# Attention probabilities: the multiply by the reciprocal sum, from VectorE to ScalarE

## The chip, the core and the metric

The kernel runs on one core of one Trainium2 chip. The metric is device time in microseconds (us), taken as the median of several runs; lower is better. The profile is of one execution on the same kind of core. The engines are called PE (TensorE, matrix products), DVE (VectorE), ACT (ScalarE), POOL (GpSimd) and SP (SyncE, which issues most of the transfers). PEld is PE's loading of weights, which overlaps its products.

## What is computed

Two blocks of a network act on x, eight batches of 512 tokens with 256 channels. Block 0 adds a state-space layer (a recurrence over time, behind several exponential moving averages) and then a mixture of 8 experts. Block 1 adds an attention layer and then a mixture of 32 experts. The change touches the attention alone:

```python
Q = (x @ Wq.T).reshape(b, n, H, R)        # H = 8 heads, R = 64
K = (x @ Wk.T).reshape(b, n, H, R)
V = (x @ Wv.T).reshape(b, n, H, d)        # d = 256
attn = jnp.einsum('bnhr,bmhr->bhnm', Q, K)
attn = jax.nn.softmax(attn, axis=-1)      # 512 x 512 for each batch and head
out = jnp.einsum('bhnm,bmhd->bnd', attn, V)
```

Everything is in 32-bit floats here.

## The kernel before

Activations lie with channels on the 128 partitions and the 512 tokens of a batch along the free axis, so a tile of 128 x 512 holds half the channels of one batch.

Two threads of work are issued interleaved. Thread X does the state-space layer, batch after batch. Its inner loop has 64 items for each batch: ACT makes dA, an exponential (line 623), POOL makes h, a product (625), DVE runs a scan along time (651) and a multiply (652), and PE folds the result (660). Beside it X does the moving averages of the next batch, scans and multiply-adds on DVE (475 to 485). Thread Y does, for a group of batches, the mixture of 8 experts and then the low-rank layer and the attention. The groups are batch 0; 1 and 2; 3, 4 and 5; 6 and 7. Y of one group runs beside X of the next. Y of the last group has no X beside it; it runs beside the routing of the second mixture (function top4). Behind all that come the 95 tiles of the 32 experts and the output. Each engine executes its instructions in the order in which they were laid down; the framework's scheduler settles that order when the program is built, from the interleaved emission, and it gives copies issued on "any" engine to ACT or DVE.

The attention of one batch runs over four pairs of heads (line 862). For each pair:

- Lines 868 to 871 make Q and K of both heads (tile qk, copied from PSUM by "any" engine).
- `scores(i)`, for each of four blocks of 128 queries and both heads u: PE makes 128 x 512 scores in a PSUM tile (888), DVE takes the row maximum nm (892), ACT takes the exponential and, in the same instruction, its row sum den (895), DVE takes the reciprocal of den (896) and multiplies ex by it in place (897). Tile ex has four buffers, den and nm have four each.
- `values(i)` makes V on PE and copies it from PSUM (879, "any" engine).
- `turn(i)` transposes ex on PE in four pieces (905) and copies the result from PSUM into aT (906, "any" engine).
- Line 922 multiplies V by aT on PE, in 32 matmul instructions a pair, and line 926 adds the sums to x.

Score tiles come from a PSUM pool g of two buffers, the values, transposes and outputs from a pool acc of two buffers. A score buffer is free again once the exponential has read it; an acc buffer once the copy has. Line 897 runs 256 times in all: 8 batches x 4 pairs x 4 blocks x 2 heads.

Of the kernel before, what the change touches and what calls it, by code (L numbers as in the profile page):

```python
# [12 lines left out]
AF = mybir.ActivationFunctionType  # L13
ALU = mybir.AluOpType
# [37 lines left out]
def adaln_attn_ffn_kernel(ctx: ExitStack, tc: tile.TileContext, d: dict, out: bass.AP):  # L52
    nc = tc.nc
# [22 lines left out]
    def mm(o, pairs):  # L76
        for i, (lhsT, rhs) in enumerate(pairs):
            nc.tensor.matmul(o, lhsT, rhs, start=(i == 0), stop=(i == len(pairs) - 1))  # L78
# [632 lines left out]
    def thread_y(q, bs, ps):  # L711
# [4 lines left out]
        def g():  # L716
            return ps.tile([P, T], F32, tag="g", name="g", bufs=2)

        def acc():
            return ps.tile([P, T], F32, tag="acc", name="acc", bufs=2)  # L720
# [94 lines left out]
        with ExitStack() as ph:  # L815
            wk = ph.enter_context(tc.tile_pool(name=f"k3_{q}", bufs=1))
            H = 8
            for r, b in enumerate(bs):
# [43 lines left out]
                for hp in range(H // 2):  # L862
                    wqk = wk.tile([P, 2, KC, P], F32, tag="wqk", name="wqk")
                    nc.sync.dma_start(wqk, d["wqk"][hp])
                    wv = wk.tile([P, KC, T], F32, tag="wv", name="wv", bufs=1)
                    nc.sync.dma_start(wv, d["Wv"][hp])
                    qk = wk.tile([P, 2, T], F32, tag="qk", name="qk")
                    for u in range(2):
                        pt = g()
                        mm(pt, [(wqk[:, u, k, :], c[:, k, :]) for k in range(KC)])  # L870
                        nc.any.tensor_copy(qk[:, u, :], pt)  # L871
                    yield 4
                    aTs = [wk.tile([P, 4, T], F32, tag=f"aT{u}", name=f"aT{u}") for u in range(2)]
                    V = wk.tile([P, 4, T], F32, tag="V", name="V")

                    def values(m):
                        pt = acc()
                        mm(pt, [(c[:, k, ts(m, P)], wv[:, k, :]) for k in range(KC)])
                        nc.any.tensor_copy(V[:, m, :], pt)  # L879

                    exs = {}

                    def scores(i):

                        sps = [g() for u in range(2)]
                        for u in range(2):
                            r0 = 64 * u
                            mm(sps[u], [(qk[r0 : r0 + 64, 0, ts(i, P)], qk[r0 : r0 + 64, 1, :])])
                        for u in range(2):
                            sp = sps[u]  # L890
                            nm = wk.tile([P, 1], F32, tag="nm", name="nm", bufs=4)
                            nc.vector.tensor_reduce(nm, sp, AX.X, ALU.max, negate=True)  # L892
                            ex = wk.tile([P, T], F32, tag="ex", name="ex", bufs=NEX)
                            den = wk.tile([P, 1], F32, tag="den", name="den", bufs=4)
                            nc.scalar.activation(ex, sp, AF.Exp, bias=nm, accum_out=den)  # L895
                            nc.vector.reciprocal(den, den)
                            nc.vector.tensor_scalar(ex, ex, den, None, ALU.mult)
                            exs[i, u] = ex

                    def turn(i):  # L900
                        for u in range(2):
                            tp = acc().rearrange("p (m t) -> p m t", m=4)
                            ex = exs.pop((i, u))
                            for m in range(4):
                                nc.tensor.transpose(tp[:, m, :], ex[:, ts(m, P)], ident)  # L905
                            nc.any.tensor_copy(aTs[u][:, :, ts(i, P)], tp)  # L906

                    for i in range(4):
                        scores(i)
                        yield 2  # L910
                        values(i)
                        yield 2
                        if i > 0:
                            turn(i - 1)
                            yield 2
                    turn(3)
                    yield 2
                    ys = [acc() for k in range(KC)]
                    for k in range(KC):
                        for u in range(2):  # L920
                            for m in range(4):
                                nc.tensor.matmul(  # L922
                                    ys[k], V[:, m, C * u + P * k : C * u + P * (k + 1)], aTs[u][:, m, :],
                                    start=(u == 0 and m == 0), stop=(u == 1 and m == 3))
                            yield 3.5
                        nc.vector.tensor_tensor(x[:, k, :], x[:, k, :], ys[k], ALU.add)
# [274 lines left out]
```

## Time and profile before

| | |
|---|---|
| median of 3 runs | 4290.34 us (4277.67 to 4293.29) |
| the profiled execution, time | 4282.53 us |
| the profiled execution, span of the page | 4280.8 us |
| mean granted PE clock | 0.886 of full speed |
| L895 on ACT, exponential, 128x512 | 256 times, 686 ns, 175.0 us |
| L896 on DVE, reciprocal, 128x1 | 256 times, 154 ns, 39.2 us |
| L897 on DVE, multiply, 128x512 | 256 times, 628 ns, 160.5 us |
| L906 on ACT, copy of aT from PSUM | 189 times, 586 ns, 108.3 us |
| L906 on DVE, copy of aT from PSUM | 67 times, 682 ns, 45.4 us |
| L879 on ACT, copy of V from PSUM | 93 times, 580 ns, 53.9 us |
| L879 on DVE, copy of V from PSUM | 35 times, 686 ns, 24.0 us |
| L623 on ACT, exponential with a scale tile | 512 times, 720 ns, 360.5 us |
| L651 on DVE, scan | 512 times, 1585 ns, 799.0 us |
| table loads on ACT | 284 |

In a line of the profile stand the source line, engine and operation, the tiles written and read with their shapes, and the count; then the busy time in us and the mean of one in ns; then the idle time of the engine just before these instructions, with the releaser that ended most of it. The rows of digits cut the span in 40 equal slices; each digit is the busy share of a slice in tenths. In the timeline a line gives start, length, engine, source line, operation and count, and in brackets the idle time before it and what ended it. One 32-bit matmul on 512 columns shows as two instructions.

### The profile page before, as it was taken

The numbers are of one execution on the slowest core, as the hardware profiler recorded it, in microseconds if no ns is written. First come the engines' busy times: TensorE is split into PE (matmuls) and PEld (weight loads), VectorE is DVE, ScalarE is ACT, GpSimd is POOL, SyncE is SP. The second block draws the span as 40 slices with busy tenths as digits, with TensorE's granted clock in tenths as the row PEclk, the third lists the DMA queues.
The fourth block names the chain that finished last, engine by engine and source line by source line (L and its number), as shares of the span: only waits on it lengthen the run. The fifth ranks groups of instructions, "written<-read, shape, count | busy, mean of one in ns | idle before, by whom it ended". The sixth has DMA issues, their size and how long they took to land. (4 is left out here: it accounts for less than half of the span.)

```text
span 4280.8 us, 36836 instructions
## 1 busy us (share of the span) xinstructions
PE 3470.1 (81%) x10964; PEld 1699.2 (40%) x10964; DVE 2667.8 (62%) x4276; ACT 1683.1 (39%) x2753; POOL 1570.6 (37%) x1222
## 2 busy tenths in 40 slices
PE   4557686888687888888858898889988999977994
PEld 2111352332254233333327443333456444436773
DVE  5698957987866686796791547565432354443336
ACT  2535463454355345346433443332223243222222
POOL 0456535435536334433552323231043211124552
PEclk7668798898798898999879998999999999989996
DMA  3325445234446423333346312213043212117776
GB/s 104 120 91 194 180 153 172 99 116 165 161 162 210 140 100 117 128 117 106 138 169 226 125 62 70 74 35 104 15 160 137 90 44 70 36 44 243 249 239 221
DMA packets 159372, 554.78 MB, mean 130 GB/s; under 512 B 27730, under 2 KB 34289, under 8 KB 146756
## 3 DMA queue, kind: packets, MB, share of 16 engines
q1 hardware_dynamic: 135076, 501.35, 34.8%
q0 software_dynamic: 24096, 51.08, 3.2%
q8 instruction: 87, 1.43, 0.1%
q14 instruction: 113, 0.93, 0.1%
HBM read 453.00 MB, written 234.82 MB: 161 GB/s over the span
## 5 line engine op out<-in xcount | busy, mean ns | idle before, releaser
L625 POOL TENSOR_TENSOR h<-packed,B 128x512 f32<-128x512 f32 x512 | 790.7, 1566 | 1045.0 <-PE yp L660 669.6
L651 DVE TENSOR_TENSOR_SCAN h<-dA,h 128x512 f32<-128x512 f32 x512 | 799.0, 1585 | 142.8 <-POOL h L625 77.3
L623 ACT ACTIVATE dA<-packed,Aexp 128x512 f32<-128x512 f32 x512 | 360.5, 720 | 676.5 <-DVE h L651 468.1
L160 POOL DMA_INDIRECT tok<-ys,to_i x310 | 312.5, 1008 | 494.4 <-DVE ys L808 228.1
L660 PE MATMUL yp<-h,fold 128*32 128x512 f32 x1024 | 355.2, 710 | 166.2 <-DVE h L652 151.8
L922 PE MATMUL acc<-aT,V 128*128 128x512 f32 x1024 | 454.4, 598 | 8.2 <-ACT aT L906 4.9
L160 POOL DMA_INDIRECT tab<-row,si x192 | 199.6, 1040 | 463.0 <-DVE si L250 170.0
L652 DVE TENSOR_TENSOR h<-h,c 128x512 f32<-128x512 f32 x512 | 329.8, 672 | 24.2 <-PE c L78 23.3
L922 PEld LDWEIGHTS acc<-aT,V 128*128 128x128 f32 x1024 | 193.2, 191 | 248.9 <-issue 236.0
L78 PE MATMUL acc<-wv,c 128*128 128x512 f32 x512 | 276.2, 655 | 2.7 <-DVE aT L906 2.0
L78 PE MATMUL g<-qk 64*128 64x512 f32 x512 | 228.2, 673 | 59.1 <-ACT qk L871 32.0
L892 DVE TENSOR_REDUCE nm<-g 128x1 f32<-128x512 f32 x256 | 170.2, 681 | 122.4 <-PE g L78 121.3
L895 ACT ACTIVATE ex<-g,nm 128x512 f32<-128x512 f32 x256 | 175.0, 686 | 163.8 <-DVE nm L892 162.6
L78 PE MATMUL g<-xT,fw 128*128 128x256 f32 x960 | 234.4, 396 | 0.4 <-ACT h L801 0.4
L78 PE MATMUL acc<-fw,h 128*128 128x256 f32 x960 | 221.6, 383 | 4.1 <-DVE ys L808 2.4
L78 PEld LDWEIGHTS g<-xT,fw 128*128 128x128 f32 x960 | 187.8, 200 | 38.7 <-issue 8.0
L905 PEld LDWEIGHTS acc<-ident,ex 128*128 128x128 f32 x1024 | 126.5, 149 | 188.1 <-issue 69.7
L78 PEld LDWEIGHTS acc<-fw,h 128*128 128x128 f32 x960 | 182.6, 192 | 42.4 <-issue 12.2
L905 PE MATMUL acc<-ident,ex 128*128 128x128 f32 x1024 | 163.8, 291 | 41.2 <-ACT V L879 26.8
L660 PEld LDWEIGHTS yp<-h,fold 128*32 128x32 f32 x1024 | 45.2, 116 | 374.4 <-DVE h L652 217.6
L479 DVE TENSOR_TENSOR_SCAN tr<-alpha,gm 128x512 f32<-128x512 f32 x128 | 182.4, 1442 | 7.4 <-POOL y L665 7.1
L78 PE MATMUL g<-xT,mw 128*128 128x256 f32 x760 | 183.9, 386 | 0.0
(280 smaller groups left out, 5437.8 us busy)
## 6 DMA issues: line engine op xcount, KB each, us to landing
fw<-in_fW SPq DMA_DIRECT2D x60, 1154.0 KB
tab<-zeros SPq DMA_DIRECT2D x32, 2112.0 KB
packed<-pack SPq DMA_DIRECT2D x128, 512.0 KB
mw<-in_mW SPq DMA_DIRECT2D x95, 384.0 KB
tab<-zeros SPq DMA_DIRECT2D x16, 2080.0 KB
xt<-tab SPq DMA_DIRECT2D x95, 264.0 KB
xz<-xzs SPq DMA_DIRECT2D x32, 512.0 KB
pack<-dd SPq DMA_DIRECT2D x32, 512.0 KB
```

Source lines behind the costliest of these rows:

```text
L78: nc.tensor.matmul(o, lhsT, rhs, start=(i == 0), stop=(i == len(pairs) - 1))
L160: i = nc.gpsimd.indirect_dma_start(out=table_, out_offset=bass.IndirectOffsetOnAxis(ap=idx, axis=0), in_=src, in_offset=None, bounds_check ...
L479: nc.vector.tensor_tensor_scan(tr, alpha[:, 1 + i : 2 + i].to_broadcast([P, T]), gm[:, k, :], 0.0, ALU.mult, ALU.add)
L623: nc.scalar.activation(dA, t[:, 0, :], AF.Exp, scale=A[:, 4 * j + k, g : g + 1])
L625: nc.gpsimd.tensor_tensor(h, t[:, 1, :], B4s[b, g], ALU.mult)
L651: nc.vector.tensor_tensor_scan(h, dAs.pop(i), h, 0.0, ALU.mult, ALU.add)
L652: nc.vector.tensor_tensor(h, h, Cs[0], ALU.mult)
L660: nc.tensor.matmul(yps[j][32 * k : 32 * k + 32, :], fold, hs.pop(i + k), start=(g == 0), stop=(g == 3))
L892: nc.vector.tensor_reduce(nm, sp, AX.X, ALU.max, negate=True)
L895: nc.scalar.activation(ex, sp, AF.Exp, bias=nm, accum_out=den)
L905: nc.tensor.transpose(tp[:, m, :], ex[:, ts(m, P)], ident)
L922: nc.tensor.matmul(ys[k], V[:, m, C * u + P * k : C * u + P * (k + 1)], aTs[u][:, m, :], start=(u == 0 and m == 0), stop=(u == 1 and m == 3))
```

## The change

The multiply of ex by the reciprocal of den goes from a tensor_scalar on VectorE to an ACTIVATE with function Identity and a per-partition scale on ScalarE. It stays in place, between the same neighbours in the code. Nothing else in the source is changed.

```diff
                             nc.scalar.activation(ex, sp, AF.Exp, bias=nm, accum_out=den)
                             nc.vector.reciprocal(den, den)
-                            nc.vector.tensor_scalar(ex, ex, den, None, ALU.mult)
+                            nc.scalar.activation(ex, ex, AF.Identity, scale=den)
                             exs[i, u] = ex
```

## The prediction

> **What bounds the kernel now.** I read the span as a whole first, then by stage. The page gives 4280.8 us; the execution it shows took 4282.53 us from outside, and the three timed runs have a median of 4290.34, so the page stands 8 us below the median.
>
> ```profile
> PE 3470.1 (81%) x10964; PEld 1699.2 (40%) x10964; DVE 2667.8 (62%) x4276; ACT 1683.1 (39%) x2753; POOL 1570.6 (37%) x1222
> DVE  5698957987866686796791547565432354443336
> ACT  2535463454355345346433443332223243222222
> L895 ACT ACTIVATE ex<-g,nm 128x512 f32<-128x512 f32 x256 | 175.0, 686 | 163.8 <-DVE nm L892 162.6
> ```
>
> On average VectorE (DVE) is not the bound, but the slices show it near full up to the middle of the span and half empty behind. The changed line works in eight attention passes of four head pairs each. The view of busy time by stage, cut at those passes (columns: stretch, length, PE, PEld, DVE, ACT, POOL busy, granted clock, DMA share, GB/s):
>
> ```profile
> 749.00:1070.00 321.00, 262.75 (x720) 98.42 (x718) 268.85 (x329) 159.17 (x255) 134.98 (x90) 0.90 0.36 127
> 1391.00:2140.00 749.00, 632.47 (x1709) 241.17 (x1710) 571.40 (x739) 354.04 (x563) 297.65 (x196) 0.90 0.35 121
> 2461.00:2889.00 428.00, 384.14 (x1107) 157.33 (x1106) 266.98 (x393) 159.39 (x309) 127.94 (x85) 0.94 0.19 60
> 2889.00:3103.00 214.00, 207.34 (x599) 87.72 (x598) 101.71 (x186) 60.72 (x130) 15.09 (x11) 1.00 0.18 60
> 3317.00:3800.00 483.00, 469.91 (x1385) 214.72 (x1386) 220.22 (x487) 152.46 (x284) 91.76 (x90) 0.97 0.18 59
> ```
>
> The first two (batches 0 to 2, beside the recurrence of thread X) have PE and DVE both near 80%: there the two take turns as the bound. In the last two PE is busy 97% of the time. A closer look at one head pair of each kind, in the timeline:
>
> ```profile
> 1538.64 2.08 PE L78 MATMUL g<-qk 64*128 64x512 f32 x4 [6.91 <-ACT qk L871]
> 1542.05 1.27 DVE L892 TENSOR_REDUCE nm<-g 128x1 f32<-128x512 f32 x2
> 1543.24 1.21 DVE L651 TENSOR_TENSOR_SCAN h<-dA,h 128x512 f32<-128x512 f32 x1
> 1549.95 1.31 DVE L897 TENSOR_SCALAR ex<-ex,den 128x512 f32<-128x512 f32 x1
> 1551.19 2.28 DVE L479 TENSOR_TENSOR_SCAN tr<-alpha,gm 128x512 f32<-128x512 f32 x1
> 1554.09 0.69 ACT L895 ACTIVATE ex<-g,nm 128x512 f32<-128x512 f32 x1 [4.49 <-DVE nm L892]
> ...
> 3055.31 0.66 PE L905 MATMUL acc<-ident,ex 128*128 128x128 f32 x4
> 3055.90 1.12 PE L78 MATMUL g<-qk 64*128 64x512 f32 x2
> 3056.95 1.98 PE L78 MATMUL acc<-wv,c 128*128 128x512 f32 x4
> ```
>
> In the first, DVE goes from one instruction to the next without a gap (32.00 of the 32 us from 1538 to 1570), ScalarE (ACT) waits for DVE and PE for ACT: what leaves DVE there can shorten the stage. In the second, PE runs gapless; its head pair takes 36.2 us, of which PE is busy 35.7.
>
> **What the Trainium skill says.** "ScalarE: Activation LUTs", section "What ACT_TABLE_LOAD costs": an ACTIVATE with one per-partition operand takes about 280 + 0.833 N ns, 707 for N = 512; the trace's ACTIVATE with a scale tile, dA on L623, took 720. Same page, section "Table sets: the hidden batching unit": identity lies in every set, so it needs no load of its own; the trace agrees, L321 runs Identity 64 times and has no table load. "SBUF — State Buffer", on the shared port pair: a DVE operation that reads one SBUF tensor through two ports excludes GpSimd for its length and the reverse. The trace fits: L897 takes 454 ns at least and 486 in the median, but 1.31 us at 1549.95 while POOL works, and 628 in the mean.
>
> **The change part by part.**
>
> *Removed from DVE:* 256 multiplies on L897, 160.5 us. By the same stage cuts: 25.8 and 46.2 us in the two mixed stretches (96 of them, 72.0 us), 35.2, 19.3 and 33.9 in the other three.
>
> *Moved back to DVE:* three tiles are copied by "any" engine, and the built program shows that the choice shifts: 77 copies leave ACT for DVE (45 of V, 28 of aT, 2 of qk, 2 of row). Only 12 of them fall in the twelve head pairs of batches 0 to 2, 25 in the next eight, and 40 in the rest. A DVE copy from PSUM takes 0.69 us. Net relief of DVE: 72.0 - 12 x 0.69 = 63.7 us in the mixed stretches, and 160.5 - 77 x 0.69 = 107 us in all.
>
> *Added to ACT:* 256 x 0.72 = 184.3 us, less 77 copies at 0.58 (44.7 us), plus 3 table loads at 1.28 (287 against 284): +143 us. In the mixed stretches: 96 x 0.72 - 12 x 0.58 = +62 us on an engine that is busy 513 of 1070 us there.
>
> *Order:* apart from these, X and Y stand against each other nearly as before (at the end of each head pair DVE has issued the same count of scans on L651, within four), and no DMA is added on SP or POOL; single loads change places with neighbours, which I put at nothing: their transfers lie beside work already waiting on engines.
>
> *What it is worth in the PE-bound stages.* I replayed the pair at 3046.7 with the new order. ACT: two exponentials, two scales, then an aT copy; DVE: two maxima, two reciprocals, a V copy, an aT copy. The first exponentials end at 3050.8; the scales run to 3051.5 and 3052.2. The next exponential then starts at 3052.24, against 3052.15 before. PE wants the first scaled tile at 3053.73, which is 2.2 us later. The tightest place is the transpose at 3055.31, which waits for the V copy on DVE: den at 3054.3, copy to 3055.04. It is met by 0.2 us. The last two scales end at 3064.3 and 3065.05; PE uses them at 3065.6 and 3066.85. So: nothing. If that cover of 0.2 us were gone, each of some 16 such pairs would lose a few tenths of a us, about 5 us in all. In the pairs from 2461 to 2889 DVE is 62% busy beside a PE at 90%: relief of 35.2 - 17 = 18 us there and 32 us more on ACT, which I take as cancelling.
>
> *What it is worth in the mixed stages.* DVE's relief of 63.7 us cannot all arrive: PE is 82 to 84% busy and takes over. Bounds: 0 if every gap is PE's or ACT's, 64 if DVE is the bound throughout. Of ACT's idle time from 749 to 1070, the waits list 89 of some 160 us as waits for DVE, and PE's own waits run to a good part over ACT; so I take half, 32 us. ACT's price: it now stands and waits for the reciprocal, which on DVE may lie behind a scan of 1.2 to 2.2 us. Queued behind it are dA, V and aT copies. dA is ahead (four buffers; ACT waited 60 us from 749 to 1070 for a free one), so only copies hurt. 48 pairs of scores, a tenth of a us each: 5 us; the upper bound is in the rival. What is late next is PE.
>
> Sum: -32 + 5 + 0 = -27 us. Against the execution shown: 4282.5 - 27 = 4255; against the median, 4290 - 27 = 4263, which is the figure I give, since runs are compared with medians.
>
> **The rivals.**
>
> *No change.* For it: PE is 81% busy overall and the granted clock in the mixed stretches is 0.90, so PE may take over at once, and ACT's waits for DVE are mostly ACT being ahead. Against: stretches such as 1538 to 1570 with DVE full and PE waiting. If a tenth of the relief arrives, 6 us, and ACT takes 5 back: 4289; with the late stages' bound, 4294. I write 4287.
>
> *ACT's queue becomes the bound (slower).* Place: the mixed head pairs. ACT executes in order; a scale waits for its reciprocal, and V, aT and qk copies behind it keep PSUM buffers from PE. Price: 48 pairs x (1.44 us of scales + about 1.3 of waiting behind a scan) = 130 us of ACT time. If half of it stands in front of something that is waited for, 65 us, against half the relief: +33, 4323. It decides from about a quarter (32 us) on. For it: before, PE waited 6.9 us for a qk copy that stood behind dA on ACT; against: ACT is only half busy there.
>
> *The port.* L897 no longer shuts GpSimd out. POOL waited 30.5 us on L897, twice, of which I believe little, because it had long been waiting for PE. If the full relief arrives and the port gives 8 more: 4290 - 64 - 8 + 5 = 4223.
>
> That the change does not do what it says is excluded: in the built program all 256 stand on ACT.
>
> **How the numbers follow.** Under 0.5% (21 us) a measurement of this kernel cannot tell from no change. Faster, as forecast: 0.44, of which 0.06 for the port; no change 0.29; ACT's queue 0.27. The faster case spans 4223 to 4269, no change up to 4311, and the rival's centre is 4323; cutting its upper part and the lowest end of the first leaves 4225 to 4330. The forecast's own range is 4235 to 4275. Chances: faster 0.44, same 0.29, slower 0.27.
>
> **What would show it.** Right: L897 on ACT at about 720 ns each, 77 copies more on DVE, DVE near 2560 us and ACT near 1826; the stretches of batches 0 to 2 shorter by some 30 us in sum; the head pairs behind 3000 still 36.2 us each with PE full. Wrong: ACT waiting long for den, PE waiting longer for V and aT copies by ACT, mixed stretches no shorter; or PE idle in the late pairs, waiting for ex.

## The result, and the profile after

The changed kernel takes 4261.14 us in the median of 8 runs (4252.34 to 4272.51), the kernel before 4283.61 in 8 runs of the same job (4276.39 to 4293.29). The ratio is 0.9947, with a 95% interval of 0.9932 to 0.9962: 22 us faster, as forecast in sign and size. The profiled execution has a span of 4254.6 us, 26.2 less than that of before, at a granted PE clock of 0.891 against 0.886.

From the page of the changed kernel: the busy times, the slices of DVE and ACT, and the group of the changed line.

```profile
PE 3468.4 (82%) x10964; PEld 1698.8 (40%) x10964; DVE 2596.7 (61%) x4097; ACT 1799.4 (42%) x2935; POOL 1580.6 (37%) x1222
DVE  4698956877956676695791547564332344443336
ACT  2535463564465457356533444343323243322222
L897 ACT ACTIVATE ex<-ex,den 128x512 f32<-128x512 f32 x256 | 175.9, 716 | 45.7 <-DVE den L896 45.2
```

The scale takes 716 ns on ACT. DVE has 71.1 us less than before, where the multiply alone was 160.5, and ACT has 116.3 more. ACT's busy time grows less than the +143 us of the prediction because the records of the scales overlap their neighbours on ACT, by 26.7 us in all; the plain sum of the lengths on ACT grows by 140. The 45 us in front of the scale are a new wait: ACT stands until DVE has made the reciprocal.

The stages can be cut where DVE copies a batch's normalised input (start of its pass) and where it adds the fourth head pair to x (end). The view of busy time by stage, for the passes of batches 0, 1 and 2 (columns as in the prediction), first before, then after:

```profile
767.52:1054.28 286.76, 237.57 (x659) 91.02 (x659) 241.92 (x300) 141.55 (x232) 115.83 (x76) 0.90 0.34 120
1480.65:1743.35 262.70, 220.41 (x607) 86.36 (x605) 213.60 (x276) 130.74 (x222) 101.94 (x67) 0.91 0.35 120
1819.72:2084.61 264.89, 228.91 (x615) 87.54 (x615) 212.66 (x275) 134.33 (x220) 101.75 (x67) 0.91 0.33 115
sum 814.35, PE 686.89 PEld 264.92 DVE 668.18 ACT 406.62 POOL 319.52; mean PE 228.96 PEld 88.31 DVE 222.73 ACT 135.54 POOL 106.51
```

```profile
765.89:1044.32 278.43, 237.44 (x654) 91.21 (x658) 225.56 (x268) 159.23 (x264) 120.51 (x76) 0.92 0.35 123
1468.90:1728.87 259.97, 221.76 (x606) 87.22 (x604) 197.33 (x251) 150.38 (x249) 102.83 (x66) 0.91 0.34 117
1814.99:2075.70 260.71, 228.86 (x611) 87.53 (x611) 202.53 (x250) 152.97 (x248) 102.75 (x65) 0.94 0.33 119
sum 799.11, PE 688.07 PEld 265.97 DVE 625.43 ACT 462.58 POOL 326.10; mean PE 229.36 PEld 88.66 DVE 208.48 ACT 154.19 POOL 108.70
```

DVE's busy time in the three passes falls by 42.8 us, the passes get 15.2 us shorter, and DVE's idle time grows by the other 27.6. PE's share rises from 84% to 86%. That DVE falls by 42.8 and not by the 72.0 of L897 has two main causes, which make up 25 of the 29 us. Copies of V and aT on DVE take 8.1 us more in the passes. And the scans of line 651 got longer; the same cuts for that line alone, before and after (columns: stretch, length, DVE busy, clock, DMA share, GB/s):

```profile
767.52:1054.28 286.76, 86.71 (x59) 0.90 0.34 120
1480.65:1743.35 262.70, 74.38 (x50) 0.91 0.35 120
1819.72:2084.61 264.89, 73.30 (x50) 0.91 0.33 115
sum 814.35, DVE 234.38; mean DVE 78.13
```

```profile
765.89:1044.32 278.43, 94.28 (x59) 0.92 0.35 123
1468.90:1728.87 259.97, 76.98 (x49) 0.91 0.34 117
1814.99:2075.70 260.71, 79.89 (x51) 0.94 0.33 119
sum 799.11, DVE 251.14; mean DVE 83.71
```

The 159 scans in the passes, as many as before, take 16.8 us more. The timeline of the changed kernel shows where such time comes from:

```profile
1540.41 4.63 POOL L625 TENSOR_TENSOR h<-packed,B 128x512 f32<-128x512 f32 x3 [0.27 <-PE yp L660]
...
1543.90 0.13 DVE L896 RECIPROCAL den<-den 128x1 f32<-128x1 f32 x1
1543.96 2.17 DVE L651 TENSOR_TENSOR_SCAN h<-dA,h 128x512 f32<-128x512 f32 x1
1544.07 0.72 ACT L897 ACTIVATE ex<-ex,den 128x512 f32<-128x512 f32 x1 [0.47 <-DVE den L896]
1546.05 0.13 DVE L896 RECIPROCAL den<-den 128x1 f32<-128x1 f32 x1
```

The median scan takes 1217 ns, this one 2170 beside POOL's products. The second reciprocal stands behind it, and the second scale on ACT behind the reciprocal. The trace bears this out for all scans: of the 201 in the whole changed kernel beside which no GpSimd instruction runs, none takes more than 1227 ns (226 and 1226 before), and in the passes the scans above 1300 ns went from 58 to 74.

The pairs of heads that run without thread X are unchanged. The last stretch of batch 5's pass, before and after (views by stage):

```profile
2970.60:3117.44 146.84, 144.65 (x421) 64.14 (x422) 61.33 (x128) 42.99 (x97) 0.00 (x0) 1.00 0.13 41
```

```profile
2951.51:3098.36 146.85, 144.66 (x421) 64.24 (x422) 54.76 (x109) 55.06 (x117) 0.00 (x0) 1.00 0.13 40
```

Not all of the gain of the passes is kept. From the end of batch 1's pass to the start of batch 2's, the changed kernel takes 86.12 us against 76.37. At the end of batch 2's pass it is only 8.9 us ahead, and the rest comes behind 2084 us. DVE's timeline in the lost stretch, first one line of before, then the changed kernel:

```profile
1793.14 0.69 DVE L838 SCALAR_TENSOR_TENSOR wi<-g,wi 128x512 f32<-128x512 f32 x1 [5.77 <-PE g L78]
```

```profile
1774.02 1.21 DVE L651 TENSOR_TENSOR_SCAN h<-dA,h 128x512 f32<-128x512 f32 x1
1788.41 0.69 DVE L838 SCALAR_TENSOR_TENSOR wi<-g,wi 128x512 f32<-128x512 f32 x1 [13.18 <-PE g L78]
1789.20 1.23 DVE L475 SCALAR_TENSOR_TENSOR gm<-gx,gated 128x1024 f32<-128x1024 f32 x1
```

No attention runs here. DVE stands 13.2 us for a product of PE, where the same line waited 5.8 at this place before, and everything laid down behind stands with it. I took this for an effect of the order of the queues, which the scheduler laid down anew for the changed program; the runs with a fixed order below bear on it. These observations leave three questions for the runs: whether DVE's relief (the time taken from it) makes the gain, what the port that it shares with GpSimd and ACT's queue have to do with it, and what the new order costs.

### The profile page after: what moved, and what is told of

Same layout as the page of the kernel before. It is cut to its first block, busy times and chain, and to the rows that moved or that the text cites. A ratio compares the mean times of both kernels' runs of the same rounds, so it can differ in the third digit from the quotient of the medians.

```text
span 4254.6 us, 36761 instructions
## 1 busy us (share of the span) xinstructions
PE 3468.4 (82%) x10964; PEld 1698.8 (40%) x10964; DVE 2596.7 (61%) x4097; ACT 1799.4 (42%) x2935; POOL 1580.6 (37%) x1222
## 5 line engine op out<-in xcount | busy, mean ns | idle before, releaser
L625 POOL TENSOR_TENSOR h<-packed,B 128x512 f32<-128x512 f32 x512 | 800.7, 1586 | 994.4 <-PE yp L660 643.7
L651 DVE TENSOR_TENSOR_SCAN h<-dA,h 128x512 f32<-128x512 f32 x512 | 822.8, 1633 | 138.2 <-POOL h L625 75.5
L660 PE MATMUL yp<-h,fold 128*32 128x512 f32 x1024 | 364.5, 703 | 157.8 <-DVE h L652 146.2
L897 ACT ACTIVATE ex<-ex,den 128x512 f32<-128x512 f32 x256 | 175.9, 716 | 45.7 <-DVE den L896 45.2
```

The source lines that it names most:

```text
L625: nc.gpsimd.tensor_tensor(h, t[:, 1, :], B4s[b, g], ALU.mult)
L651: nc.vector.tensor_tensor_scan(h, dAs.pop(i), h, 0.0, ALU.mult, ALU.add)
L660: nc.tensor.matmul(yps[j][32 * k : 32 * k + 32, :], fold, hs.pop(i + k), start=(g == 0), stop=(g == 3))
L897: nc.scalar.activation(ex, ex, AF.Identity, scale=den)
```

## Experiments

All ratios are to the kernel before, run on the same chip in the same job, with 95% intervals.

### Only the early batches, only the late ones

Against the changed kernel:

```diff
-                            nc.scalar.activation(ex, ex, AF.Identity, scale=den)
+                            if q < 2:
+                                nc.scalar.activation(ex, ex, AF.Identity, scale=den)
+                            else:
+                                nc.vector.tensor_scalar(ex, ex, den, None, ALU.mult)
```

q < 2 are batches 0 to 2, 96 of the 256 scales; the second kernel has q >= 2.

> The multiply is on ScalarE for the groups of batches 0 to 2 (96 of 256) and on VectorE for the rest. My theory, that the gain comes from VectorE relieved where the recurrence runs beside attention: 0.9935 to 0.997 of the time before (12 to 28 us less), the pass ends of batch 2 earlier than before. If the gain arises in the late groups: 0.998 to 1.001.

> The multiply is on ScalarE for the groups of batches 3 to 7 (160 of 256) and on VectorE before. My theory: 0.998 to 1.001, head pairs with no recurrence beside them 36.2 us as before. If the late groups carry the gain, as the profile after suggests for about half of it: 0.996 to 0.998.

Early alone: 4254.63 us, ratio 0.9954 (0.9936 to 0.9973). Late alone: 4269.05 us, ratio 0.9979 (0.9968 to 0.9990). The first lies in the range of my theory. The second lies just outside it, and inside the alternative's at its upper edge. Most of the gain comes from the batches beside the recurrence, about 20 of 22 us. The late part is not worth nothing, as the prediction had it, but some 0.2%; together the two give slightly more than the whole change, within the intervals. Both kernels are laid down anew, so the split holds the effect of two new orders too. In its profile e1_mixonly is 9.4 us ahead of before at the end of batch 2's pass and 26.1 at the end of batch 7's, though none of its scales stands behind batch 2: a gain behind that pass needs no late scale.

### No multiply at all

```diff
                             nc.vector.reciprocal(den, den)
-                            nc.vector.tensor_scalar(ex, ex, den, None, ALU.mult)
                             exs[i, u] = ex
```

> The multiply by the reciprocal sum is left out on both engines, so the attention is not normalised. What ScalarE's new work costs is then absent: if ScalarE's price is about 5 us, as forecast, 0.991 to 0.9945 of the time before; if ScalarE's queue eats half of the relief, below 0.989.

The normalisation is left out, and all queues are laid down anew. Measured: 4269.86 us, ratio 0.9994 (0.9981 to 1.0006), outside both ranges. No gain, though both engines have less to do than before (DVE 2554.2 us busy, ACT 1676.3). In the profile the kernel is 22 us ahead at the start of batch 1's pass and 3 us behind three head pairs later. Part of it shows where DVE stands at its additions to x (line 925 in this kernel, 926 in before), first the longest such wait of before in this pass, then e3_noscale:

```profile
1589.82 0.69 DVE L926 TENSOR_TENSOR x<-x,acc 128x512 f32<-128x512 f32 x1 [7.67 <-PE acc L922]
```

```profile
1566.77 0.69 DVE L925 TENSOR_TENSOR x<-x,acc 128x512 f32<-128x512 f32 x1 [5.54 <-PE acc L921]
1579.44 0.69 DVE L925 TENSOR_TENSOR x<-x,acc 128x512 f32<-128x512 f32 x1 [11.98 <-PE acc L921]
```

These waits come to 19 us in that pass, against 9 before; the other 15 us of the loss I did not trace. Work left out changes the order too, so this run can't tell a worthless relief from a bad order. The next ones hold the order fixed.

### More work on ScalarE

```diff
-                    nc.vector.tensor_scalar(dd[:, 0, :], pt, col("bdt", j), 0.0, ALU.add, ALU.max)
+                    nc.scalar.activation(dd[:, 0, :], pt, AF.Relu, bias=col("bdt", j))
...
-                    nc.vector.tensor_scalar(u, e, 1.0, None, ALU.add)
+                    nc.scalar.activation(u, e, AF.Identity, bias=one)
...
-                    nc.vector.tensor_scalar(c2[:, e, :], pt, cb[:, e : e + 1], None, ALU.add)
+                    nc.scalar.activation(c2[:, e, :], pt, AF.Identity, bias=cb[:, e : e + 1])
```

These edits stand on top of the change.

> As the changed kernel, and three more operations of VectorE go to ScalarE: the bias and rectifier of the step sizes (L560, 32 times), the addition of one (L563, 32 times), the bias of the expert layer (L743, 16 times), about 63 us of VectorE. If VectorE's relief beside the recurrence goes on to pay at a third to a half: 0.985 to 0.992 of the time before. If ScalarE's queue or PE has become the bound: 0.994 to 1.005.

Measured: 4298.01 us, ratio 1.0055 (1.0038 to 1.0072): slower than before, and just beyond both ranges. DVE is busy for 2554.0 us, 43 less than in the changed kernel, ACT for 1838.4. Between the start of batch 1's pass and that of batch 2's the kernel loses 28 us against before, half of it by the third head pair of batch 1, the stretch in which e3_noscale lost. Whether ACT's load or the order did it isn't told apart by this run. It shows that less time on DVE isn't a gain by itself.

### The order held fixed: short multiplies, and the control

Here the program is built as it is, and only then are single instructions exchanged in place, so that every queue keeps its order and its waits. Where instructions are cut short or replaced, the normalisation is left out in whole or in part; the routing behind the attention then sees other values, but the three passes lie ahead of it.

```diff
     with tile.TileContext(nc) as tc:
         adaln_attn_ffn_kernel(tc, args, out)
...
+                if s.debug is not None and s.debug.lineno == 897:
+                    kind = dict(op0=s.op0, op1=s.op1) if hasattr(s, "op0") else dict(func=s.func)
+                    ops[j] = type(s)(name=s.name, engine=s.engine, ins=[narrow(p) for p in s.ins],
+                                     outs=[narrow(p) for p in s.outs], sync_info=s.sync_info, debug=s.debug, **kind)
```

narrow gives an operand of 512 columns 8 columns. The first kernel has this on before, the second on the changed kernel, the third is before, unchanged.

> The kernel before in its own order, instruction for instruction on every engine; only the 256 multiplies on L897 (VectorE) are cut from 512 to 8 columns after the order has been laid down, so the normalisation reaches 8 columns alone. About 145 of VectorE's 160.5 us go, nothing is added to ScalarE, and no instruction moves. Theory 1 (relief of VectorE in the passes of batches 0 to 2 is what makes the time, and e3_noscale lost it again to the order that was laid down anew there): 30 to 50 us faster than before, ratio 0.988 to 0.993, and no loss in the passes of batches 1 and 2. Theory 2 (VectorE's relief is worth nothing by itself, and the changed kernel gained by the order it was given): within 12 us of before, ratio 0.997 to 1.001, as e3_noscale.

> The changed kernel in its own order; only the 256 scales on L897 (ScalarE) are cut from 512 to 8 columns after the order has been laid down, so the normalisation reaches 8 columns alone. Some 100 us of ScalarE go and no instruction moves: what this gains over the changed kernel (ratio 0.9947 to before) is the price of the scales on ScalarE. Theory 1 (the price is small, the 5 us of the prediction): ratio 0.992 to 0.995. Theory 2 (ScalarE's queue takes back a good part of the relief, 20 us or more): ratio 0.990 or below, gained in the passes of batches 0 to 2.

> The kernel before, unchanged, profiled a second time: how far the ends of the attention passes stand apart in two executions of the same program. Both theories: every pass within 2 us of the first profile, so that the differences of 4 to 20 us between the kernels are differences of the programs. If single passes differ by 5 us or more, the stage figures of single profiles tell little.

f1_short_dve: 4248.67 us, ratio 0.9921 (0.9901 to 0.9941), 34 us faster, in the first theory's range. In before's order the relief arrives. The relief was smaller than I had expected, 67.4 us of DVE's busy time and not 145, because 8 columns still cost 231 ns in the median. One line's view by source, in f1_short_dve (durations: min/median/max in ns):

```profile
L897 DVE TENSOR_SCALAR ex<-ex,den x256: 199/231/2168, 781.0 to 3744.3; 128x8 f32<-128x8 f32 x128
```

The three passes of this kernel, and then the sum over those of e3_noscale:

```profile
764.43:1044.66 280.23, 235.18 (x659) 90.61 (x659) 233.50 (x300) 141.34 (x232) 116.20 (x76) 0.91 0.34 123
1473.13:1729.14 256.01, 219.52 (x607) 86.77 (x605) 205.87 (x276) 130.80 (x222) 104.19 (x67) 0.92 0.35 123
1805.56:2066.26 260.70, 226.57 (x615) 86.62 (x615) 203.06 (x276) 134.14 (x220) 100.47 (x67) 0.92 0.33 117
```

```profile
sum 811.67, PE 681.48 PEld 266.05 DVE 610.99 ACT 404.10 POOL 320.17; mean PE 227.16 PEld 88.68 DVE 203.66 ACT 134.70 POOL 106.72
```

DVE has 25.8 us less there, and the passes are 17.4 us shorter, more than the 15.2 of the changed kernel with its relief of 42.8. And e3_noscale, with 57.2 us less on DVE in the passes, won 2.7. Both take time of the multiply from DVE and add nothing to ACT; e3_noscale takes more of it, and what sets it apart is the program laid down anew: the order of its queues, and with it the engine of some copies. I put what it lost down to that; no run tests a single place of the order.

f2_short_act: 4254.06 us, ratio 0.9940 (0.9919 to 0.9962), against 0.9947 of the changed kernel. With 97 us less on ACT, in the same order, the passes are 2.2 us shorter (796.88 against 799.11), no more than such sums differ by. So the length of the scales costs a few us at most. What this run leaves in place is the wait: its scales still stand for their reciprocals, 65.1 us in all. Two views speak for a small price of that wait. PE and PEld waited for the scaled tiles 25.4 us in the changed kernel and 22.8 before (view by source of L897). And PE does not stand longer in front of the score products (first before, then after):

```profile
L78 PE MATMUL g<-qk 64*128 64x512 f32 x512 | 228.2, 673 | 59.1 <-ACT qk L871 32.0
```

```profile
L78 PE MATMUL g<-qk 64*128 64x512 f32 x512 | 229.1, 676 | 52.6 <-ACT ex L895 38.3
```

But PE's waits for exponentials, which can stand behind the scales on ACT, grew: between the start of batch 0's pass and the end of batch 2's they are 17.4 us before (22.9 when before is profiled again) and 29.1 after. A price of several us for the wait in ACT's queue is not excluded.

The stretch between batches 1 and 2 takes 84.37 us here too, so the loss of 10 us there isn't the scales' length either. Its length goes with the order: it takes 76.4 to 81.5 us in the seven profiles with before's order (before, f1_short_dve, f3_before_again and, from further below, g1_one_port, g2_more_dve_before, h1_accum_all and h2_accum_early), and 84.4 to 86.1 us in the three with the changed kernel's (the changed kernel, f2_short_act and g3_more_dve_after).

f3_before_again: 4287.3 us in one run, passes 812.93 against 814.35 us. Up to the end of batch 2's pass the milestones lie within 6 us of the first profile, most within 3; then the stretch from 2084 to 2481 us differs by 8.5 us between the two executions of one program. My "within 2 us" was too narrow. Sums over the passes are good to a few us. The 6.6 us that the changed kernel gains in the stretch from 2084 to 2481 us can't be told from this spread.

### The port, and time given back to VectorE

The port is the shared one that the prediction cites: over it, a multiply on VectorE and work on GpSimd exclude each other. With the same exchange in place, RED being the row maximum of line 892:

```diff
+                    src, dst = cols(s.ins[0], 352), cols(s.outs[0], 1)
+                    ops[j] = type(RED)(name=s.name, engine=s.engine, ins=[src], outs=[dst], op=RED.op, axis=RED.axis,
+                                       sync_info=s.sync_info, debug=s.debug)
```

This is line 897 in before's order, so that the probabilities stay without their scale. The two others exchange line 896, with 400 columns of ex as source and den as result, in before's order and in the changed kernel's.

> The kernel before in its own order; each of the 256 multiplies on L897 is replaced, after the order has been laid down, by a maximum over 352 columns of the same tile in the same place of VectorE's queue: about as long as the multiply (486 ns in the median), but it writes one column[...]. The normalisation is left out. Theory 1 (VectorE's time is what counts): within 10 us of before, ratio 0.998 to 1.002, against 0.992 of f1_short_dve. Theory 2 (the port: L897 shut GpSimd out, and that is what the change took away): as fast as f1_short_dve, ratio 0.990 to 0.995, with GpSimd's products on L625 shorter than 1566 ns in the mean.

> The kernel before in its own order; each of the 256 reciprocals on L896 (154 ns) is replaced, after the order has been laid down, by a maximum over 400 columns of the exponentials (an estimated 0.55 us), so that VectorE has about 100 us more work, all of it in the score tiles. The multiply then scales by that maximum and not by the reciprocal sum. Theory 1 (about half of what stands on VectorE there reaches the time): 40 to 65 us slower than before, ratio 1.009 to 1.015. Theory 2 (VectorE has room, and f1 gained by a shorter path from the exponential to the transposes alone): below 25 us, ratio under 1.006.

> The changed kernel in its own order, with the same replacement of the 256 reciprocals on L896 by maxima over 400 columns: VectorE gets back about the 107 us that the change took from it net, in the changed kernel's order and with the scales on ScalarE. The scales use that maximum and not the reciprocal sum. Theory 1 (the gain is VectorE's relief): the gain of 22 us is gone and some more, since ScalarE also waits longer for the result: ratio 1.000 to 1.008. Theory 2 (the gain is the order that the change happened to get, or the port): it stays, ratio 0.994 to 0.997.

g1_one_port: 4253.17 us, ratio 0.9929 (0.9910 to 0.9947), as fast as f1_short_dve. The first theory's number is missed, the second's is met. But the reason that the second gave isn't there. The line by source, in before and in g1_one_port:

```profile
L897 DVE TENSOR_SCALAR ex<-ex,den x256: 454/486/2435, 784.1 to 3774.4; 128x512 f32<-128x512 f32 x128
```

```profile
L897 DVE TENSOR_REDUCE ex<-ex x256: 486/515/521, 784.9 to 3738.9; 128x1 f32<-128x352 f32 x128
```

The median is 29 ns longer, but the tail of long ones is gone, and with it 29.8 us of busy time: the 256 take 130.7 us instead of 160.5. GpSimd's products on line 625 are no shorter (1572 ns, before 1566). In before's trace 53 of the 256 multiplies take more than 550 ns, and a GpSimd instruction runs beside every one of them; of the 171 with none beside, the longest takes 489. So the port cost VectorE its own time. Of the 160.5 us of line 897, 256 x 0.486 = 124.4 us were its own length and some 36 us were waiting, 25 of them in the three passes (72.0 - 96 x 0.486). The waiting stood where DVE is full: the passes have 23.1 us less of DVE and are 25.8 us shorter. The sums over the passes of g1_one_port, g2_more_dve_before and g3_more_dve_after:

```profile
sum 788.56, PE 675.57 PEld 262.09 DVE 645.05 ACT 405.76 POOL 326.42; mean PE 225.19 PEld 87.36 DVE 215.02 ACT 135.25 POOL 108.81
```

```profile
sum 828.68, PE 693.19 PEld 266.25 DVE 696.88 ACT 407.41 POOL 323.64; mean PE 231.06 PEld 88.75 DVE 232.29 ACT 135.80 POOL 107.88
```

```profile
sum 826.04, PE 701.01 PEld 268.90 DVE 656.33 ACT 465.88 POOL 317.83; mean PE 233.67 PEld 89.63 DVE 218.78 ACT 155.29 POOL 105.94
```

g2_more_dve_before: 4306.96 us, ratio 1.0058 (1.0038 to 1.0078). DVE has 84.3 us more in all, in the passes 28.7, and these are 14.3 us longer. The kernel is 25 us slower, which misses the first theory's 40 to 65 and meets the second's figure at its edge: of time added all over the kernel less than a third arrives, of time added in the passes half. The second theory's reason, a shorter path from the exponential to the transposes, doesn't hold all the same: the maximum (560 ns in the median) lengthens that path by 0.4 us a tile, f2_short_act shortened it by as much in 256 places by cutting the scale, and won 2.2 us in the passes.

g3_more_dve_after: 4291.21 us, ratio 1.0023 (1.0011 to 1.0034). Its busy times:

```profile
PE 3484.5 (81%) x10964; PEld 1704.2 (40%) x10964; DVE 2689.1 (63%) x4097; ACT 1808.5 (42%) x2935; POOL 1569.8 (37%) x1222
```

With 92 us given back to DVE, somewhat more than the 71 that the change had taken, the gain is gone and 10 us more. Order, scales on ACT and the absence of line 897 from DVE are those of the changed kernel. The path through the scale is 0.4 us longer a tile here as well, which by f2_short_act is worth little. So neither the order nor the free port as such made it faster; the time that DVE got did.

### One port with the whole computation

```diff
-                            nc.vector.tensor_scalar(ex, ex, den, None, ALU.mult)
+                            nc.vector.tensor_scalar(ex, ex, den, None, ALU.mult, op1=ALU.add, accum_out=den)
```

The second kernel has it for q < 2 alone. In both, every queue keeps the order of before; on DVE a reading of the sum stands behind each such multiply.

> The kernel before in its own order on every engine; the multiply on L897 stays on VectorE with all 512 columns, but in the form that also sums its result (into den, which nothing reads after it). [...]From the maxima over 352 and 400 columns (515 and 560 ns) 512 columns should take an estimated 0.67 us, without the long tail up to 2.4 us: about 170 us in all against 160.5, and about 64 against 72 in the passes of batches 0 to 2. Theory 1 (only VectorE's time counts, the wait at the port being part of it): -8 us there, up to +9 in the other stages: within 10 us of before, ratio 0.998 to 1.002. Theory 2 (the lock of L897 costs beyond VectorE's own time, so that g1_one_port gained by its absence): 20 us or more faster, ratio 0.993 to 0.996, though VectorE is busy as long as before.

> As h1_accum_all, but the summing form is used only in batches 0 to 2 (96 of the 256 multiplies), where GpSimd works beside VectorE; the other 160 keep the 486 ns of the plain form. A real version that keeps the whole computation. Theory 1: 5 to 12 us faster than before, ratio 0.997 to 0.999. Theory 2: 20 to 28 us, ratio 0.993 to 0.995, as fast as the changed kernel or better.

h1_accum_all: ratio 0.9991 (0.9978 to 1.0003). h2_accum_early: 0.9991 (0.9975 to 1.0006). The first theory's range holds for the first; its 5 to 12 us for the second came out at about 4. (The medians are 4313.37 and 4306.43 us, against 4313.91 of the kernel before in this job; before itself is some 30 us slower here than in the other jobs, so only the ratios are read.) The line by source in h2_accum_early:

```profile
L897 DVE TENSOR_SCALAR_CACHE_REDUCE ex<-ex,den x96: 710/733/747, 785.8 to 2053.9; 128x512 f32<-128x512 f32 x96
L897 DVE DVE_READ_ACCUMULATOR ex<-ex,den x96: 72/77/85, 786.5 to 2054.5; 128x1 f32 x96
```

The tail is gone here as well, but the form is 247 ns longer than the plain multiply's median. (The reading of its sum adds nothing to that: in the timeline it starts before the multiply ends, together with the next instruction of DVE.) The passes hold 70.7 us of it instead of 72.0, and there is no gain to be seen in the time. Had shutting out GpSimd cost 20 us beyond DVE's own time, as the second theory said, it would have shown; that is outside the interval. A smaller cost is not excluded: the second interval reaches to 11 us, and in these two profiles the passes take 801.4 and 804.4 us against 814.35 before, with DVE's busy time within 3 us of before's. Those profiles are of another job, of which before has none, so this stays open. In the main the port matters as part of the multiply's length. On this, the Trainium skill, "SBUF — State Buffer", section "Who interferes with whom", says which instructions of DVE compete with GpSimd: a multiply by a scalar in its two-port form, and one with two SBUF inputs against a GpSimd operation that reads SBUF, but not a reduction, and not the form that also writes its accumulator. The runs agree for all four: 2435 ns at most for the multiply, a scan of 2170 beside GpSimd against 1217 in the median, 521 at most for the maximum, 748 for the summing form (h1_accum_all).

No kernel of these that keeps the whole computation beats the changed one; e1_mixonly is as fast (0.9954 against 0.9947).

## Why the prediction was right

In sum it was: 4263 us forecast, 4261.14 measured. Step by step:

- *DVE bounds the mixed stages, and what leaves it shortens them.* Shown, from both sides and with the order fixed: 0.67 us of pass for each us taken (f1_short_dve), 1.1 for the waits at the port (g1_one_port), 0.5 for each us added to before (g2_more_dve_before), 0.87 for each added to the changed kernel (g3_more_dve_after). Half, which I took, lies at the low end. A value above 1 is more than DVE's own time can give, so a few us of spread, or something beside that time, are in it.
- *Removed 72.0 us in the mixed stretches, 77 copies back.* Right: DVE's copies of V went from 35 to 80 and of aT from 67 to 95, 8.1 us more in the passes where 12 x 0.69 = 8.3 had been put.
- *Net relief of 63.7 us.* This is the term that was mis-sized: it was 42.8, and over the whole kernel 71.1 instead of 107. The 628 ns of the multiply's mean held a wait for GpSimd, some 25 us of the 72.0 in the passes. I had seen the 1.31 us beside the 486 ns, but counted the wait as work that goes away with the instruction. The scans of line 651 got 16.8 us longer in the same passes. With the order fixed they didn't (f1_short_dve -2.0 us, g1_one_port +1.9), so it belongs to the new order, in which a scan meets GpSimd more often: 74 scans above 1300 ns in the passes, 73 and 66 in the two other kernels with this order, against 53 to 62 in all with before's. That these are waits beside GpSimd the trace shows; that they are the multiply's own waits, moved to the scan, wasn't tested.
- *Half of it arrives, 32 us in the mixed stages.* The passes gained 15.2, which is 0.36 of the 42.8 and not half; by the 0.67 of f1_short_dve it should have been 29, and whether the new order or ACT's waits took the rest isn't told apart. And 9.8 were given back between batches 1 and 2, which no step of mine had. The working took the order as unchanged, since it counted scans at the ends of head pairs; such a count doesn't show a single wait of DVE for PE. How much a newly laid order can take is shown by e3_noscale against f1_short_dve: 34 us won with before's order, 3 without.
- *ACT's price, 5 us.* The length of the scales costs about 2 us in the passes (f2_short_act). The forecast was of the wait for the reciprocal, and that wait is real, 45 us on ACT. PE's waits for the scaled tiles hardly grew, so most of it looks free, but its price was not measured.
- *Nothing in the pairs without thread X.* Right: 146.85 against 146.84 us for four pairs.
- *From 2461 to 2889 us relief and ACT's load cancel.* Wrong by a little: late scales alone give 0.2% (e2_lateonly), and f1_short_dve gains 8.8 us from 2481 to 2970.
- *The sum of -27.* The spans differ by 26.2 us, the medians by 22.5. That the sum fits is in good part luck: the profile is 8.9 us ahead at the end of batch 2's pass, where 27 were forecast, and 17 come behind it, where nothing was. Too much in the mixed stages stood against too little behind them. Part of the gain behind 2084 us is of the size by which two profiles of one program differ, and where that part comes from stays open.

The rivals: no change is excluded by the interval. (Its figure of 4287 doesn't follow from its own working, which gives 4289 to 4294; nothing hangs on it.) ACT's queue as the bound, with 65 us lost, did not come: the changed kernel is faster, and shorter scales win 2.2 us. It may begin with the further load of e4_moreact, which isn't settled. The port, to which I gave 0.06, had its place wrong: GpSimd's products got no shorter, and little was rightly made of the 30.5 us that it "waited on L897". But the wait at the port lay on VectorE's side, and to be rid of that wait alone (g1_one_port) is worth as much as the whole change.

## What to carry to other kernels

When an instruction is to leave an engine, look at its minimum, median and maximum and not only at its mean: here what lay above the median was waiting, and such a wait may show up again at another instruction that wants the same port. To price an instruction, keep the order of all queues and make it short in place; to leave it out and build anew also changes the order, and here that was worth as much as the change itself, as far as e3_noscale and f1_short_dve tell. Before a stage's difference is explained, profile the same program twice.

## What the runs showed of the hardware that was not expected

- A VectorE multiply of 8 columns takes 231 ns in the median, of 512 columns 486: nearly half the length doesn't depend on the size. The wait for GpSimd does not shrink with it either: 2168 ns at most with 8 columns, 2435 with 512.
- Maxima over 352 and 400 columns in SBUF take 515 and 560 ns in the median, so each further column adds an estimated 0.94 ns; over 512 columns from PSUM (line 892) 681.
- The multiply that also sums its result takes 741 ns in the median for 512 columns, where the plain one takes 486. The reading of the sum has a record of 82 ns of its own, but DVE's next instruction starts with it.
